# Cross-attention deviations turned ahead of the scores, context statistics paced one step sooner, one third of a pair's queries moved to the step before; the last expert's full block ahead of its short part

## The chip, the cores and the metric

The kernel runs on one core of a Trainium2 chip. Its time is device microseconds of one launch; before the change three runs gave a median of 565.46 us (563.95 to 566.39). The profile is one further execution of the same kernel, taken with the hardware profiler.

Five engines work side by side, each through its own list of instructions in the order in which it was built: PE (matrix multiply), DVE (vector), ACT (activation), POOL, and SP, which here only issues DMA. They meet through semaphores. In the profile PEld is PE's loading of weights.

## The reference, cut to what matters

One Perceiver layer on 1024 query rows (32 batches of 32, width 512), all in float32:

```python
xn  = layernorm(x)                                  # no weights
x1  = layernorm(xn) * g1 + b1;  x2 = layernorm(ctx) * g2 + b2   # ctx: 32 x 257 x 384
q   = x1 @ Wq + bq;  k = x2 @ Wk + bk;  v = x2 @ Wv + bv
x   = x + softmax(q @ k.T * 512**-0.5) @ v @ Wo + bo            # cross-attention
x   = x + self_attention(layernorm(x))              # 16 heads of 32, rotary positions
xf  = layernorm(x)
s, e = top_k(sigmoid(xf @ gate.T + bias), 2);  s = s / (s.sum(-1) + 1e-6)
x   = x + sum_j s_j * (silu(xf @ w1[e_j].T) @ w2[e_j].T)        # 8 experts, 1024 wide
```

## The kernel before, in words

**Folded weights.** The cross-attention's key weights are folded into the query weights (`mq`), its value and output weights into one (`wvo`). Scores are then taken on the raw context, and each key's reciprocal deviation (`rs`, one number for each of 257 keys) multiplies them afterwards.

**Eight steps.** A step `g` treats four batches, that is 128 query rows (tile `g` of `x_sb`). Two steps form a pair `p = g // 2`; queries are made for a whole pair. The loop at the end of the cross-attention runs `g` from 0 to 8 and overlaps neighbours: step `g` takes the scores of `g` and finishes the mixing of `g - 1`. On PE a step holds these groups:

- `pte` (L588): the weights `ex` of step `g - 1` transposed; ACT copies them to `eT` (L590).
- `pscore` (L542): the scores of `g`, from the queries `q2T` and the transposed context `nT`.
- `pc` (L599): `eT` times the context `n`; DVE evicts it to `u` (L606).
- `prs` (L557): the spread deviations `rx` of `g` transposed; ACT copies them to `rb` (L560). DVE then multiplies the scores by `rb` and takes the maximum in one custom instruction (`ex`, L563), followed by `mxq`, `nm`, ACT's exponential (L576) and DVE's product with `rb` (L579).
- `ptu` (L624), copied to `uT` (L626), and `po` (L633), which DVE adds to `x_sb` (L636).
- In even steps `pt` (L446): the next pair's normalized rows `y` transposed to `x1T`. In odd steps `pq`, `pbt` and `pb` (L475, L467, L484): the next pair's queries, three columns blocks `c` of four matmuls each. Late steps hold pieces of the self-attention's first pair instead (`spt`, `pp`).

**Statistics.** `cstats(g)` makes the deviations of step `g`: nine `bn_stats` on DVE (L505; eight on `n`, one on the last key `nl`), five small operations ending in `v` (L517), a power on POOL (`rs`, L519), and ACT's copies to `rx` and `rb` (L526, L532). It is called in step `g - 1`. `pace` holds instructions that others are to be issued after: `cstats(g)` goes after `pace["c", g]`, which before the change is the eviction `u` of step `g - 2`, executed in step `g - 1`.

**Context loads.** `load_ctx(g)` loads `n` (four DMAs of 384 KB, one per batch), `nl` (four of 48 KB) and `nT` (1542 KB), all on SP's queue; it is called three steps ahead, in `xmix(g - 3)`. Buffers: steps 2 and 5 lie in the pool `ewp`, the others alternate between two. SP waits before an issue until the buffer is free[...].

**What sets the order.** A scheduler in the framework places each engine's instructions, and DMAs on SP, from the program text, priorities and its own estimates; the text's order is not the built order. Where this document speaks of the built order, it was read from the built programs.

**Experts.** After self-attention and routing, the experts run one after the other, the fullest first. Rank `r` takes `WIDTH[r]` rows of its list: full blocks of 128 rows and a remainder that `short_part` treats in packed form (L1311 to L1317). `output` does the short part first, then the full blocks (L1397 to L1403). Each eviction `fob` is added to the rows of `out` by an indirect accumulating DMA on POOL (`add_rows`, L194). These DMAs all write `out`, so each waits for the one before. Unused places of a block point to 128 spare rows behind the 1024 real ones.

Of the kernel before, what the change touches and what calls it, by code (L numbers as in the profile page):

```python
# [9 lines left out]
F32 = mybir.dt.float32  # L10
# [7 lines left out]
P = 128  # L18
# [17 lines left out]
WIDTH = (384, 352, 288, 288, 288, 224, 192, 160)  # L36
CAP = max(WIDTH)
NB = CAP // P
EARLY = 2
Q = 32  # L40
YI, YC, YW = D, D + 8, D + 16
# [10 lines left out]
def tile_perceiver_layer(  # L52
# [138 lines left out]
        nc.vector.bn_aggr(mv, st)  # L191

    def add_rows(dst, ob, place, n):
        nc.gpsimd.indirect_dma_start(  # L194
            out=dst,
            out_offset=bass.IndirectOffsetOnAxis(ap=place, axis=0),
            in_=ob,
            in_offset=None,
            bounds_check=n * (NTT * P + P) - 1,
            oob_is_err=True,  # L200
            compute_op=ALU.add,
        )
# [22 lines left out]
    with ExitStack() as attn:  # L225
# [19 lines left out]
        with ExitStack() as xa:  # L245
# [209 lines left out]
                        )  # L455
                qs[p]["x1T"] = x1T

            def xquery(p):

                x1T = qs[p]["x1T"]  # L460
                q2T = wk.tile([P, KC, 2 * P], F32, tag="q2T", name="q2T")
                for c in range(KC):
                    if c == KC - 1:

                        pb = ps.tile([P, D], F32, tag="ps", name="pbt")
                        for k in range(KD):
                            nc.tensor.matmul(  # L467
                                pb[ts(k, Q), 0 : 2 * P], mq[:, k, DX - Q : DX], x1T[:, k, :],
                                start=True, stop=True,
                            )  # L470
                        pbs = wk.tile([P, 2 * P], F32, tag="eT", name="pbs")
                        nc.scalar.copy(pbs, pb[:, 0 : 2 * P])
                    pq = ps.tile([P, D], F32, tag="ps", name="pq")
                    for k in range(KD):
                        nc.tensor.matmul(  # L475
                            pq[:, 0 : 2 * P], mq[:, k, ts(c, P)], x1T[:, k, :],
                            start=(k == 0), stop=(k == KD - 1),
                        )
                    nc.scalar.activation(
                        q2T[:, c, :], pq[:, 0 : 2 * P], AF.Identity, bias=tcol[:, c : c + 1]  # L480
                    )
                pb = ps.tile([P, D], F32, tag="ps", name="pb")
                for i in range(2):
                    nc.tensor.matmul(  # L484
                        pb[:, i : i + 1], pbs[:, ts(i, P)], copies[:, 0, 0, Q - 1 : Q],
                        start=True, stop=True,
                    )
                qb = spool.tile([P, 2], F32, tag="qb", name="qb")
                nc.vector.tensor_scalar_add(qb, pb[:, 0:2], tcol[:, KC : KC + 1])
                qs[p]["q2T"], qs[p]["qb"] = q2T, qb  # L490

            def xbias(p):
                for i in range(2):
# [53 lines left out]
                        )  # L547
                gs[g]["pscore"] = pscore

            def xweights(g):  # L550

                p, i = g // 2, g % 2
                qb, rb, pscore = qs[p]["qb"], gs[g]["rb"], gs[g]["pscore"]

                pr = ps2.tile([P, 2, P], F32, tag="pt", name="prs")
                for c in range(2):
                    nc.tensor.transpose(  # L557
                        pr[:, c, :], gs[g]["rx"][:, c].rearrange("p b q -> p (b q)"), ident
                    )
                nc.scalar.copy(rb[:, 0:NK], pr.rearrange("p c k -> p (c k)"))  # L560
                ex = wk.tile([P, S], F32, tag="ex", name="ex")
                mx = spool.tile([P, 1], F32, tag="mx", name="mx")
                top = nc.vector.tensor_tensor_reduce(  # L563
                    out=ex, in0=pscore[:, 0:S], in1=rb, scale=1.0, scalar=-3.0e38,
                    op0=ALU.mult, op1=ALU.max, accum_out=mx,
                )
                if g % 2 or g == 0:
                    pace["x", p + 1 + g % 2] = top.ins
                mq_ = spool.tile([P, 1], F32, tag="mq", name="mxq")
                nc.vector.tensor_tensor(mq_, mx, qb[:, i : i + 1], ALU.add)  # L570
                nm = spool.tile([P, 1], F32, tag="nm", name="nm")
# [21 lines left out]
            def xmix(g):  # L593

                n, nl, ex, eT = gs[g]["n"], gs[g]["nl"], gs[g]["ex"], gs[g]["eT"]
                pc = ps.tile([P, D], F32, tag="ps", name="pc")
                for c in range(2):
                    for b in range(4):
                        nc.tensor.matmul(  # L599
                            pc[ts(b, T), 0:DC],  # L600
                            eT[:, c, ts(b, T)],
                            n[:, b, c, :],
                            start=(c == 0), stop=(c == 1),
                        )
                u = wk.tile([P, DC], F32, tag="u", name="u")
                mixed = nc.vector.scalar_tensor_tensor(  # L606
                    u, nl, ex[:, NK : NK + 1], pc[:, 0:DC], op0=ALU.mult, op1=ALU.add
                )
# [20 lines left out]
            def xout(g):  # L629
                uT = gs[g]["uT"]  # L630
                po = ps.tile([P, D], F32, tag="ps", name="po")
                for c in range(KC):
                    nc.tensor.matmul(  # L633
                        po, uT[:, c, :], wvo[:, c, :], start=(c == 0), stop=(c == KC - 1)
                    )
                nc.vector.scalar_tensor_tensor(  # L636
                    x_sb[:, g, :], po, gs[g]["rc"], x_sb[:, g, :],
                    op0=ALU.mult, op1=ALU.add,
                )


            DX = DC + 1
# [98 lines left out]
            for g in range(NTT + 1):  # L741
# [524 lines left out]
    def tails_of(m):  # L1266

        return [(0, 2 * Q)] * (m // (2 * Q)) + [(m // Q * Q - Q, Q)] * (m // Q % 2)
# [34 lines left out]
    def short_part(hT, w2, q, place, sh):  # L1303
# [13 lines left out]
        add_rows(out.rearrange("r (n w) -> (r n) w", n=n), ob[:, 0:w], place, n)  # L1317

    def turn_rows(r, xs, n, taken, idx):

# [58 lines left out]
                nc.tensor.transpose(pt[:, k, :], t["hs"][:, ts(h * KD + k, P)], ident)  # L1379
            evac(h, t["hT"][:, h * KD : (h + 1) * KD, 0:P], pt)  # L1380

    def output(t, w2):

        hT, share, idx = t["hT"], t["share"], t["idx"]
        parts = parts_of(t["n"])
        for c, m in parts:
            if m < P:
                for r0, q in tails_of(m):
                    short_part(
                        hT[:, :, c * P + r0 : c * P + r0 + q], w2, q, *t["spread"].pop(0)  # L1390
                    )
        for c, m in parts:
            if m < P:
                continue
# [5 lines left out]
                )  # L1400
            ob = fw.tile([P, D], F32, tag="fob", bufs=3, name="fob")
            nc.vector.tensor_scalar_mul(ob, po, share[:, c : c + 1])  # L1402
            add_rows(out, ob, idx[:, c : c + 1], 1)  # L1403


    rows_of = {
# [8 lines left out]
    for r in range(1, NE):  # L1415
# [8 lines left out]
        if r == 1:  # L1424
# [139 lines left out]
```

## Time and profile before

| | |
|---|---|
| median of three runs | 565.46 us (563.95 to 566.39) |
| the profiled execution's own time | 566.19 us |
| its span in the profile | 564.5 us |
| granted PE clock over the span | 0.975 |
| busy: PE, DVE, ACT, POOL | 525.1, 254.0, 123.2, 83.5 us |
| cross-attention's overlapped steps 1 to 7 | 44.3 to 126.8 us |
| last matmul ends; last add is issued; it lands | 553.3; 554.4; 559.2 us |

The span runs from the first to the last instruction of the program; the profiled execution's own time is 1.7 us longer, for what lies around it. It was 0.7 us above the median of the three runs. In lines of groups, "x" counts instructions as the trace records them: a float32 matmul of this kernel stands as two records, so a block of four `pq` matmuls is "x8". In the timeline a line gives start, length, engine, source line, operation, what it writes and reads, and in brackets the engine's idle time before it with its releaser.

### The profile page before, as it was taken

The page shows a single profiled execution, that of the slowest core. Times are in us where ns is not written, and L with a number is a line of the kernel's source. Part 1 is how long each engine was busy: PE and PEld are TensorE (multiplying, and loading weights), DVE is VectorE, ACT ScalarE, POOL GpSimd, SP SyncE. Part 2 cuts the span into 40 slices and gives each one's busy share as a digit, 9 for nine tenths or more (in the row PEclk, how much of TensorE's full clock was granted, in tenths as well). Part 3 has the DMA queues.
Part 4 walks back from the last instruction along what each step waited for, and adds up shares of the span by engine and source line. Part 5 has one row for each costly group of instructions (what it writes and reads, how often), then busy time and mean ns, then how long its engine had stood idle before and what let it go on. Part 6 is the DMA issues. An engine that isn't in the chain of part 4 may idle for free.

```text
span 564.5 us, 11301 instructions
## 1 busy us (share of the span) xinstructions
PE 525.1 (93%) x4716; PEld 340.8 (60%) x4716; DVE 254.0 (45%) x758; ACT 123.2 (22%) x274; POOL 83.5 (15%) x120
## 2 busy tenths in 40 slices
PE   6999797999999999998969999999999999999992
PEld 3646354566584875776548456547657475768580
DVE  6657778747567765668534032203122121222220
ACT  3534444323313312212022021002011010102010
POOL 2110221110001012021302110122120202112211
PEclk9999999999999999798989999999999999999997
DMA  8999979999910002012295341657553554746421
GB/s 281 383 372 395 318 244 324 357 387 386 384 58 38 3 24 93 2 42 76 81 381 216 90 100 69 238 133 221 167 168 111 128 198 154 215 159 197 161 27 21
DMA packets 43086, 104.51 MB, mean 185 GB/s; under 512 B 3985, under 2 KB 7185, under 8 KB 42002
## 3 DMA queue, kind: packets, MB, share of 16 engines
q1 hardware_dynamic: 38434, 94.91, 46.8%
q0 software_dynamic: 4592, 8.78, 7.7%
q8 instruction: 39, 0.64, 0.5%
q14 instruction: 21, 0.17, 0.1%
HBM read 75.50 MB, written 28.18 MB: 184 GB/s over the span
## 4 chain that ended last, share of the span: by engine, by line
PE 69%; DVE 2%; issue 1%; ACT 1%; POOL 0%; POOLq 0%; ACTq 0%
PE ph L1344 18%; PE fpo L1397 15%; PE pp L380 8%; PE ppv L818 5%; PE ppo L894 4%; PE fpq L1311 4%; PE phe L1148 3%; PE poe L1162 2%; PE pg L940 2%; PE pos L875 2%; PE pqs L833 2%; PE phb L1365 1%; PE xpt L1326 1%; ACT xT L176 1%; PE fpt L931 1%
## 5 line engine op out<-in xcount | busy, mean ns | idle before, releaser
L1344 PE MATMUL ph<-xT,w 128*128 128x288 f32 (+4 forms) x448 | 100.2, 382 | 3.1 <-ACT xT L176 3.1
L1344 PEld LDWEIGHTS ph<-xT,w 128*128 128x128 f32 x448 | 79.0, 190 | 19.6 <-ACT xT L176 3.7
L1397 PE MATMUL fpo<-w,hT 128*128 128x512 f32 x192 | 84.4, 596 | 0.0
L1397 PEld LDWEIGHTS fpo<-w,hT 128*128 128x128 f32 x192 | 35.9, 190 | 43.9 <-issue 43.7
L1350 DVE TENSOR_TENSOR hT<-ph,sg 128x288 f32<-128x288 f32 (+4 forms) x56 | 23.6, 422 | 61.7 <-ACT sg L1349 61.7
L1402 DVE TENSOR_SCALAR fob<-fpo,share 128x512 f32<-128x512 f32 x12 | 9.0, 751 | 77.0 <-PE fpo L1397 77.0
L1349 ACT ACTIVATE sg<-ph 128x288 f32<-128x288 f32 (+4 forms) x56 | 21.5, 383 | 85.0 <-PE ph L1344 83.5
L505 DVE BATCH_NORM_STATS2 st<-n 128x6 f32<-128x384 f32 x64 | 32.7, 549 | 2.1 <-DMA n<-in_ctx_dram 2.1
L194 POOL DMA_INDIRECT out_dram<-fob,idx x12 | 18.5, 1542 | 93.7 <-DVE fob L1402 80.9
L176 ACT COPY xT<-xpt 128x512 f32<-128x512 f32 (+2 forms) x12 | 6.0, 496 | 112.5 <-PE xpt L1326 112.4
L894 PE MATMUL ppo<-ao,oT 128*128 128x512 f32 x64 | 30.1, 624 | 0.0
L194 POOL DMA_INDIRECT out_dram<-fob,plc x9 | 13.9, 1541 | 101.5 <-DVE fob L1316 84.9
L519 POOL TENSOR_TENSOR rs<-v,mhalf 128x9 f32<-128x9 f32 x8 | 14.4, 1798 | 80.7 <-DVE v L517 42.6
L380 PE MATMUL pp<-syT,aq 128*128 128x256 f32 x96 | 25.7, 427 | 0.0
L633 PE MATMUL po<-wvo,uT 128*128 128x512 f32 x48 | 22.4, 602 | 1.2 <-ACT uT L626 1.2
L818 PE MATMUL ppv<-av,syT 128*128 128x512 f32 x48 | 23.3, 635 | 0.0
L475 PE MATMUL pq<-x1T,mq 128*128 128x256 f32 x96 | 23.1, 385 | 0.0
L1311 PE MATMUL fpq<-w,hT 128*32 128x128 f32 (+1 forms) x576 | 22.3, 309 | 0.0
L380 PE MATMUL pp<-syT,ak 128*128 128x256 f32 x96 | 22.3, 385 | 0.0
L1032 POOL DMA_INDIRECT xs_d<-fy,pi x16 | 17.0, 1064 | 35.3 <-DVE pi L1028 21.9
L380 PEld LDWEIGHTS pp<-syT,aq 128*128 128x128 f32 x96 | 20.2, 216 | 3.3
L894 PEld LDWEIGHTS ppo<-ao,oT 128*128 128x128 f32 x64 | 12.6, 199 | 14.2 <-issue 14.0
(269 smaller groups left out, 732.5 us busy)
## 6 DMA issues: line engine op xcount, KB each, us to landing
xs_d<-zero SPq DMA_DIRECT2D x8, 2112.0 KB, 20.5
w<-in_w1T_dram SPq DMA_DIRECT2D x16, 1024.0 KB, 8.4
w<-in_w2T_dram SPq DMA_DIRECT2D x16, 1024.0 KB, 8.2
nT<-in_ctxT_dram SPq DMA_DIRECT2D x8, 1542.0 KB, 9.6
n<-in_ctx_dram SPq DMA_DIRECT2D x32, 384.0 KB, 7.0
xs<-xs_d SPq DMA_DIRECT2D x4, 528.0 KB, 9.3
x_sb<-in_x_dram SPq DMA_DIRECT2D x8, 256.0 KB, 6.7
out_dram<-x_sb SPq DMA_DIRECT2D x8, 256.0 KB, 2.0
```

What stands on the lines that cost most here:

```text
L194: nc.gpsimd.indirect_dma_start(out=dst, out_offset=bass.IndirectOffsetOnAxis(ap=place, axis=0), in_=ob, in_offset=None, bounds_check=n * ( ...
L380: nc.tensor.matmul(pp[:, i, :], w[:, k, ts(e, P)], yT[:, k, :], start=(k == 0), stop=(k == KD - 1),)
L475: nc.tensor.matmul(pq[:, 0 : 2 * P], mq[:, k, ts(c, P)], x1T[:, k, :], start=(k == 0), stop=(k == KD - 1),)
L505: nc.vector.bn_stats(st[:, r, :], n[:, r // 2, r % 2, :] if r < 8 else nl)
L633: nc.tensor.matmul(po, uT[:, c, :], wvo[:, c, :], start=(c == 0), stop=(c == KC - 1))
L818: nc.tensor.matmul(pp, st[p]["yT"][:, k, ts(i, P)], av[:, k, :], start=(k == 0), stop=(k == KD - 1),)
L894: nc.tensor.matmul(pp, st[p]["oT", i][:, k].rearrange("p b q -> p (b q)"), ao[:, k, :], start=(k == 0), stop=(k == KD - 1),)
L1311: nc.tensor.matmul(po[ts(g, Q), 0:w], hT[:, f, ts(h, Q)], w2[:, f, ts(j, w)], start=(f == 0), stop=(f == KF - 1),)
L1344: nc.tensor.matmul(ph[:, 0:n], w1[:, k, ts(f, P)], t["xT"][:, k, 0:n], start=(k == 0), stop=(k == KD - 1),)
L1349: nc.scalar.activation(sg[:, 0:n], ph[:, 0:n], AF.Sigmoid)
L1350: nc.vector.tensor_mul(hT[:, f, 0:n], ph[:, 0:n], sg[:, 0:n])
L1397: nc.tensor.matmul(po, hT[:, f, ts(c, P)], w2[:, f, :], start=(f == 0), stop=(f == KF - 1),)
```

## The change

It has five parts.

1. **Deviations ahead of the scores.** The transposes `prs` and their copy to `rb` leave `xweights` for a new function `xdev(g)`, called before `xscores(g)`.
2. **Statistics one step sooner.** `pace["c", g + 3]` becomes the addition of `po` to `x_sb` in `xout(g)`, in place of `pace["c", g + 2]` at the eviction `u` in `xmix(g)`. `cstats(3)` to `cstats(7)` may thus be issued from the end of the step before the one that held them. `cstats(2)` keeps its place after `u` of step 0.
3. **A third of the queries.** `xquery` takes a range of column blocks. Block 0 is called at the end of the even step, after `xout`; blocks 1 and 2 stay in the odd step.
4. **`xbias`** is called one step later, after `xquery` and `xnorm`.
5. **Last expert.** `output` gets `short_first`; the last expert does its full block first and its short part after, and its two DMAs are declared independent. For that the spare rows become 384, one set of 128 for each block (`ROWS`, `idx`), and the output tensor grows from 1152 to 1408 rows.

```diff
+ROWS = NTT * P + NB * P
 def add_rows(dst, ob, place, n):
-    nc.gpsimd.indirect_dma_start(
+    return nc.gpsimd.indirect_dma_start(
...
-        bounds_check=n * (NTT * P + P) - 1,
+        bounds_check=n * ROWS - 1,
-            def xquery(p):
+            def xquery(p, cs=range(KC)):
...
-                for c in range(KC):
+                for c in cs:
...
+                if cs[-1] < KC - 1:
+                    return
-            def xweights(g):
-
-                p, i = g // 2, g % 2
-                qb, rb, pscore = qs[p]["qb"], gs[g]["rb"], gs[g]["pscore"]
-
+            def xdev(g):
+
+                rb = gs[g]["rb"]
                 pr = ps2.tile([P, 2, P], F32, tag="pt", name="prs")
                 for c in range(2):
                     nc.tensor.transpose(
                         pr[:, c, :], gs[g]["rx"][:, c].rearrange("p b q -> p (b q)"), ident
                     )
                 nc.scalar.copy(rb[:, 0:NK], pr.rearrange("p c k -> p (c k)"))
+
+            def xweights(g):
+
+                p, i = g // 2, g % 2
+                qb, rb, pscore = qs[p]["qb"], gs[g]["rb"], gs[g]["pscore"]
...
-                pace["c", g + 2] = mixed.ins
+                if g == 0:
+                    pace["c", 2] = mixed.ins
...
+                pace["c", g + 3] = added.ins
...
+                    xdev(g)
                     xscores(g)
...
                     if g % 2 == 0:
                         xturn(p + 1)
-                        xbias(p + 1)
                     else:
-                        xquery(p + 1)
+                        xquery(p + 1, range(1, KC))
                         if p + 2 < NTT // 2:
                             xnorm(p + 2)
+                        xbias(p + 1)
...
                 if g:
                     xout(g - 1)
+                if g % 2 == 0 and p + 1 < NTT // 2:
+                    xquery(p + 1, range(1))
...
-        idx, pattern=[[0, NE], [0, LIST // P]], base=NTT * P, channel_multiplier=1
+        idx, pattern=[[0, NE], [P, LIST // P]], base=NTT * P, channel_multiplier=1
...
-    def output(t, w2):
+    def output(t, w2, short_first=True):
...
+        if short_first:
+            short()
         for c, m in parts:
             if m < P:
                 continue
...
+        if not short_first:
+            short()
+
+            for i, a in enumerate(adds):
+                for b in adds[:i]:
+                    tc.declare_no_dep(a.ins, b.ins, reason="rows of their own")
...
-        output(t, w2s.pop(r))
+        output(t, w2s.pop(r), r + 1 < NE)
```

More of the change, by code (lines that the diff above doesn't have):

```diff
@@ L456, in xturn @@
                 qs[p]["x1T"] = x1T
-            def xquery(p):
+            def xquery(p, cs=range(KC)):
                 x1T = qs[p]["x1T"]
-                q2T = wk.tile([P, KC, 2 * P], F32, tag="q2T", name="q2T")
-                for c in range(KC):
+                if cs[0] == 0:
+                    qs[p]["q2T"] = wk.tile([P, KC, 2 * P], F32, tag="q2T", name="q2T")
+                q2T = qs[p]["q2T"]
+                for c in cs:
                     if c == KC - 1:
@@ L489, in xquery @@
                 nc.vector.tensor_scalar_add(qb, pb[:, 0:2], tcol[:, KC : KC + 1])
-                qs[p]["q2T"], qs[p]["qb"] = q2T, qb
+                qs[p]["qb"] = qb
             def xbias(p):
@@ L635, in xout @@
                     )
-                nc.vector.scalar_tensor_tensor(
+                added = nc.vector.scalar_tensor_tensor(
                     x_sb[:, g, :], po, gs[g]["rc"], x_sb[:, g, :],
@@ L1316, in short_part @@
         nc.vector.tensor_scalar_mul(ob[:, 0:w], po[:, 0:w], sh)
-        add_rows(out.rearrange("r (n w) -> (r n) w", n=n), ob[:, 0:w], place, n)
+        return add_rows(out.rearrange("r (n w) -> (r n) w", n=n), ob[:, 0:w], place, n)
     def turn_rows(r, xs, n, taken, idx):
@@ L1380, in turn_hidden, with short @@
             evac(h, t["hT"][:, h * KD : (h + 1) * KD, 0:P], pt)
-    def output(t, w2):
+    def output(t, w2, short_first=True):
         hT, share, idx = t["hT"], t["share"], t["idx"]
         parts = parts_of(t["n"])
[L1386 to L1391, printed above, removed]
+        adds = []
+        def short():
+            for c, m in parts:
+                if m < P:
+                    for r0, q in tails_of(m):
+                        adds.append(
+                            short_part(
+                                hT[:, :, c * P + r0 : c * P + r0 + q],
+                                w2, q, *t["spread"].pop(0),
+                            )
+                        )
+        if short_first:
+            short()
         for c, m in parts:
@@ L1402, in output @@
             nc.vector.tensor_scalar_mul(ob, po, share[:, c : c + 1])
-            add_rows(out, ob, idx[:, c : c + 1], 1)
+            adds.append(add_rows(out, ob, idx[:, c : c + 1], 1))
+        if not short_first:
[3 more added lines that the diff above has]
+                    tc.declare_no_dep(a.ins, b.ins, reason="rows of their own")
     rows_of = {
@@ L1557 @@
     args["out"] = nc.dram_tensor(
-        "out_0_dram", (NTT * P + P, D), F32, kind="ExternalOutput"
+        "out_0_dram", (ROWS, D), F32, kind="ExternalOutput"
     ).ap()
```

## The prediction, made before the changed kernel had run

> **What bounds the kernel now.** Read first the page's busy line, then PE's waits from 40 to 140 us, then PE's timeline of one step, then the context tile's view and the table by stage. PE is busy for 93% of the span:
>
> ```profile
> PE 525.1 (93%) x4716; PEld 340.8 (60%) x4716; DVE 254.0 (45%) x758; ACT 123.2 (22%) x274; POOL 83.5 (15%) x120
> ```
>
> So time is won only where PE waits, and a wait added ahead of PE costs its full length. The change touches two places: the cross-attention's steps (44.3 to 126.8 us) and the last 12 us. In the first, PE's waits (total us, times, longest) are:
>
> ```profile
> PE prs L557 <- ACT rx L526: 4.3, 3, 1.9
> PE ptu L624 <- DVE u L606: 2.1, 2, 1.7
> PE pc L599 <- ACT eT L590: 1.9, 2, 1.7
> PE po L633 <- ACT uT L626: 1.2, 2, 1.0
> ```
>
> That is 9.5 us; 1.0 of it (`po` of step 8) isn't touched, which leaves 8.5. Step 3 on PE shows the form:
>
> ```profile
> 66.45 0.38 PE L588 MATMUL pte<-ident,ex 128*128 128x128 f32 x2
> 66.76 1.51 PE L542 MATMUL pscore<-nT,q2T 128*32 128x257 f32 x24
> 68.08 1.47 PE L599 MATMUL pc<-n,eT 128*32 128x384 f32 x16
> 71.44 0.44 PE L557 MATMUL prs<-ident,rx 128*128 128x128 f32 x2 [1.88 <-ACT rx L526]
> 71.72 1.03 PE L475 MATMUL pq<-x1T,mq 128*128 128x256 f32 x4
> ```
>
> `prs` stands third, behind 2.7 us of `pscore` and `pc`, and still waits 1.88 us for `rx`. The deviations are late; where `prs` stands is not the cause. `rx` waits for POOL's power, and that for DVE's statistics:
>
> ```profile
> 69.16 1.80 POOL L519 TENSOR_TENSOR rs<-v,mhalf 128x9 f32<-128x9 f32 x1 [10.88 <-DVE v L517]
> ```
>
> From the end of `v` to `prs` this is 0.1 + 1.8 + 0.4 + 0.1 = 2.4 us. The statistics need the context `n`, and here the DMA queue is full: the table by stage gives for steps 1 and 2 (last columns PE clock, DMA share, GB/s), and the tile's view the time from issue to landing:
>
> ```profile
> 44.27:56.88 12.61, 12.61 (x91) 8.04 (x90) 11.01 (x32) 4.41 (x11) 1.06 (x1) 1.00 1.01 393
> 56.88:66.45 9.57, 7.53 (x63) 3.79 (x61) 6.71 (x18) 5.50 (x13) 1.39 (x2) 1.00 0.91 310
> DMA to landing us min/median/max: 3.3/7.0/14.8
> ```
>
> The 14.8 us is the last of the four loads of `n(3)`: issued at 49.6, landed at 64.3; the first two landed at 60.6 and 62.2. DVE began `cstats(3)` at 62.5, just after.
>
> [...] at 82.6 us `eT` starts only after `rx` and `rb`, which waited for POOL until 82.2. [...] The landings agree; between 44 and 66 us they follow the issues at about 0.39 MB a microsecond. [...] The trace shows such waits (up to 4.8 us), and independent spare rows are what lets the last two adds go without one.
>
> **The change part by part.** In the built order every step begins `pte`, `prs`, `pscore`, `pc` (steps 5 and 7: `prs` after 5 and 9 of 12 score matmuls). I walk the steps with each engine's built order and the durations of the trace before.
>
> *Removed and added instructions:* none but order. A block of four `pq` costs 1.8 us (1.99 less overlap); one block moves from steps 1, 3, 5 to 0, 2, 4. PE's sum stays. Behind `pt` in step 0 it waits for nothing: `x1T` ends at 45.5, and its fourth matmul starts at 45.6. So step 1 starts at 46.1 (before 44.3) and step 2 at 57.0 (before 56.9): cost 0.
>
> *`prs` first, step 2.* `cstats(2)` keeps its pace after `u`, which DVE now runs after the scores' maximum and two `bn_stats` of 0.6 on `x_sb`, at 49.8 (before 47.4). Two `bn_stats` (0.48) and the product bring it to 51.8, six more and `nl` to 55.2, the small ones to 56.1; POOL takes the pair's power (0.7) first, then this (1.8): 58.6. `rx` ends at 59.0, so `prs` waits from 57.3 to 59.1: 1.8 us. Queued behind it on PE are `pscore` and `pc`; on ACT `rx` holds back two `y` (1.5) and `eT`, so `pc` starts at 60.9 (before 60.4). The old wait of 1.67 on `eT` has only changed its name.
>
> *Statistics sooner, step 2.* DVE's built order now has three `bn_stats` on `n(3)` ahead of the maximum of step 2, the fourth and fifth ahead of `u`. The third needs the second load of `n(3)`. But SP's built order puts all four loads of `n(5)` ahead of `nT(4)` and `n(3)`; before it was two. That is 0.79 MB more in a full queue, 2.0 us: the second load lands at 64.2 (60.6 + 2, 62.2 + 2 for the first two), the third at 65.2. DVE waits; maximum 64.4, `u` 65.8 to 66.4, `ptu` 66.4 (before 62.6). PE waits 4.1 us in place of 0.37. Then `pt` 0.9, `uT` (after the exponential, as built) 67.7, `po` 2.7, moved `pq` 1.8: step 3 starts at 72.2, before 66.45 + 1.8: 3.9 late.
>
> *Step 3.* DVE ends `cstats(3)` at 70.7, `rx` 73.0: `prs` waits 0.5 in place of 1.88. No other wait; seven `bn_stats` of `n(4)` (landed by 71.8 as before) end at 74.7, when the scores do. Step 4 starts at 83.6, before 81.0: 2.6 late.
>
> *Step 4.* POOL gives `rs` at 82.4, so `prs` waits for nothing. But ACT's order now has `rx`, `q2T`, two `y` and two `pair` (3.0 us) ahead of `eT`, which ends at 86.4; `pc` waits 1.0. On DVE two `xrow` additions wait for the `y` reads, one `row` addition for `pair`; with the addition to `x_sb` and two `bn_stats` the maximum comes at 87.7, `u` at 89.0 to 89.6, `ptu` waits 1.7 (before 1.70). Step 5: 95.5 against 90.5 + 1.8: 3.2 late.
>
> *Steps 5 to 7.* `v` of 5 and 7 is built behind DVE's addition of the `po` that closes the step before, so `rx` comes 2.3 to 3.2 us into the step: `prs` waits 1.6 and 2.0, with `pscore`'s rest, `pc` and, in 7, `pp` behind it, which used to fill that time (1.39, 1.03). Step 6: `uT` behind the exponential, `po` waits 1.1 (0.25). Starts of 6, 7, 8: 107.9, 116.2, 131.7 against 104.7, 112.4, 126.8: **4.9 late**. In sum 14 us of waits against 8.5; the rest of the difference is rounding of 0.1 a step.
>
> *`xbias` later:* four DVE additions of 0.6 beside waiting time; where they matter (step 4) they are counted.
>
> *Last expert.* PE ends at 553.3 either way. Before:
>
> ```profile
> 553.36 0.75 DVE L1402 TENSOR_SCALAR fob<-fpo,share 128x512 f32<-128x512 f32 x1 [6.68 <-PE fpo L1397]
> 554.38 1.54 POOL L194 DMA_INDIRECT out_dram<-fob,idx  x1 [5.89 <-DVE fob L1402]
> ```
>
> Its add lands at 559.2, 4.8 after issue. After: `fpo` ends 1.9 earlier, its add is issued at 552.4 and lands at 557.3. The short eviction takes 0.35 (553.75); POOL is free at 554.0; a short add lands 3.4 after issue: 557.4 to 557.6 behind the other's packets. **Saved 1.6 us**; bounds 0.4 (the short add takes 4.8 after all) and 1.9 (both overlap fully). `fpo` starting right after `ph` needs the last `hT` only in its eighth pair, 6 us later: 0.
>
> **Sum:** +4.9 - 1.6 = +3.3 us. Self-attention starts that much later and PE runs through, so nothing returns it. Against the profiled execution's own 566.19 us: 569.5. That execution stood 0.7 above the median of the runs shown, 565.46; so 568.8.
>
> **Rivals.**
> - *`n(3)` is in time* (a load lands by 61 us, or DVE's gap is filled): step 2's `ptu` waits 0.8, step 4 starts at 80.4, 3.2 less late, and the rest follows. +1.7 - 1.6: 565.6. For it: the loads' issue times could shift. Against: 393 GB/s and the built order of SP.
> - *The waits go* (ends faster): DVE gets so far ahead that `rx` is ready when `pte` ends in each step. Then the 4.3 us of `prs` and 0.25 of `po` vanish and `pc` and `ptu` keep theirs: -4.5 - 1.6: 559.3. It decides where `v` ends 2.4 us before a step does. For it: from step 3 on `cstats` may start a step sooner, and DVE is busy 69 of 96 us here. Against: `v` of 5 and 7 stands behind `po`'s addition in the built order, and `n(3)` can't come sooner.
> - *More is late:* `nT(7)` now goes ahead of `n(6)` on SP, 4 us of queue; if `n(6)` and `n(7)` miss their earlier `bn_stats` too, 2 us each more: 573.
>
> A built order that left the old one standing is excluded: it has changed on four engines.
>
> **How the numbers follow.** About 0.5% (2.8 us) is what a measurement of this kernel can tell from no change. Chances: the walk 0.50, `n(3)` in time 0.27, waits go 0.15, more late 0.08. The walk's centre lies 0.5 us beyond the bound; it leaves out every wait that it doesn't list, so I count 0.36 of its 0.50 as slower, 0.14 as no change. The second gives 0.22 no change, 0.03 faster, 0.02 slower; the third 0.14 faster, 0.01 no change. Slower 0.46, same 0.37, faster 0.17. The walk's own range is 566.5 to 571; with the others, the tail's bounds and 2 in 10 left out, 561.5 to 572.5.
>
> **What would show it.** Right: `ptu` of step 2 idle about 4 us for `u`, DVE just before it idle for DMA `n`; `prs` waits of 1 to 2 us in steps 2, 5, 7; step 8's `pte` near 131.7; `n(3)` landing from 62.6; the last short add landing near 557.5 plus the delay. Wrong: DVE waits on `n` below 1 us, or PE's waits on `rx` gone.

## The result, and the profile after

The changed kernel took 572.29 us (median; 569.67 to 574.14) where the kernel before took 565.82 beside it: ratio 1.0119, interval 1.0082 to 1.0156, that is 6.5 us slower. Executed again on a chip together with other kernels it took 570.43 against 565.53: ratio 1.0087 (1.0055 to 1.0118), 4.9 us slower. The forecast was 568.8, 3.3 us slower than the shown median. The direction held, and so did the range, whose upper end was 572.5; the size was too small.

PE is as full as before, so the loss must again be read from its waits. First the busy line of the changed kernel's page, then its PE waits from 40 to 140 us (total us, times, longest; `po` of step 8 lies outside):

```profile
PE 530.1 (93%) x4716; PEld 343.9 (60%) x4716; DVE 254.3 (45%) x758; ACT 123.0 (22%) x274; POOL 83.4 (15%) x120
```

```profile
PE prs L560 <- ACT rx L531: 5.1, 4, 1.7
PE ptu L633 <- DVE u L614: 3.8, 2, 2.1
PE po L642 <- ACT uT L635: 0.7, 1, 0.7
PE pc L607 <- ACT eT L598: 0.6, 1, 0.6
```

That is 10.2 us against 8.5 for the same waits before; the forecast had 14. The timeline of step 2, cut to PE and DVE, shows the wait that the prediction put in the middle of its sum:

```profile
62.44 1.50 PE L607 MATMUL pc<-n,eT 128*32 128x384 f32 x16
62.51 1.55 DVE L510 BATCH_NORM_STATS2 st<-n 128x6 f32<-128x384 f32 x3 [2.81 <-DMA n<-in_ctx_dram]
...
63.97 0.41 DVE L571 CUSTOM_DVE_ANT_0 ex<-pscore,rb 128x257 f32<-128x257 f32 x1
...
65.41 0.60 DVE L614 SCALAR_TENSOR_TENSOR u<-nl,ex,pc 128x384 f32<-128x384 f32 x1
...
66.06 0.33 PE L633 MATMUL ptu<-ident,u 128*128 128x128 f32 x1 [2.13 <-DVE u L614]
```

DVE stands 2.81 us before the first of three `bn_stats` on `n(3)` (the forecast had it stand at the third); the maximum (`ex`) and `u` are behind them in DVE's order, and PE's `ptu` waits for `u`. The table by stage for step 2 (PE clock, DMA share, GB/s last) shows the same full queue as before:

```profile
58.75:71.62 12.87, 9.20 (x70) 5.31 (x69) 9.78 (x27) 5.29 (x13) 2.65 (x2) 1.00 0.94 325
```

At the end, POOL's last two adds and DVE's eviction ahead of the last one:

```profile
559.80 1.54 POOL L195 DMA_INDIRECT out_dram<-fob,idx  x1 [15.99 <-DVE fob L1424]
561.88 1.54 POOL L195 DMA_INDIRECT out_dram<-fob,plc  x1 [0.54 <-DVE fob L1329]
```

```profile
561.25 0.35 DVE L1329 TENSOR_SCALAR fob<-fpq,shq 128x128 f32<-128x128 f32 x1 [1.73 <-PE fpq L1324]
```

PE ends at 560.61 and the span at 570.6: 10.0 us, against 11.2 before (553.31, 564.5). The tail saves 1.2. Over all profiles below, this time is 10.0 to 10.6 us in thirteen of the fourteen with the new tail (11.5 in one) and 11.0 to 11.2 in the six without it.

The second execution of the same kernel differs in step 2. DVE's first statistics of `n(3)` there, and PE behind them:

```profile
63.52 1.02 DVE L510 BATCH_NORM_STATS2 st<-n 128x6 f32<-128x384 f32 x2 [5.02 <-DMA n<-in_ctx_dram]
```

```profile
67.26 0.90 PE L633 MATMUL ptu<-ident,u 128*128 128x128 f32 x3 [4.51 <-DVE u L614]
67.95 1.91 PE L447 MATMUL pt<-ident,y 128*128 128x128 f32 x8
```

The load was later, the wait was 4.5 us, and behind it PE's instructions are longer than elsewhere in the steps: three `ptu` 0.90 us where 0.55 is usual, eight `pt` 1.91 where 1.04. The table by stage gives that step a PE clock of 0.90, not 1.00:

```profile
57.55:74.37 16.82, 10.76 (x71) 6.60 (x69) 9.85 (x27) 5.95 (x15) 3.23 (x2) 0.90 0.89 312
```

PE busy 10.76 for the work that took 9.20 in the first profile: 1.56 us went to the clock, which stood at half from 67.1 to 70.5 us. Such a stretch at half clock is named *a stretch* below.

Behind the steps the two profiles differ in the clock too. The table by stage for self-attention and routing, first of the kernel before, then of the first and the second profile of the changed one (PE clock third from the end):

```profile
137.00:256.00 119.00, 116.33 (x1915) 81.86 (x1916) 79.21 (x164) 28.94 (x55) 14.05 (x29) 0.96 0.25 93
256.00:310.00 54.00, 47.67 (x682) 33.58 (x681) 28.63 (x118) 12.44 (x23) 11.52 (x19) 0.91 0.50 192
...
137.00:256.00 119.00, 115.34 (x1922) 82.86 (x1922) 76.64 (x162) 29.51 (x57) 10.60 (x27) 0.96 0.28 103
256.00:310.00 54.00, 47.66 (x659) 30.94 (x658) 29.45 (x108) 11.54 (x21) 11.03 (x18) 0.84 0.50 188
...
137.00:256.00 119.00, 114.98 (x1946) 80.95 (x1945) 80.15 (x167) 30.98 (x60) 12.49 (x28) 1.00 0.32 115
256.00:310.00 54.00, 47.63 (x663) 31.74 (x662) 29.73 (x117) 11.29 (x20) 9.88 (x17) 0.84 0.47 178
```

### The profile page after: what moved, and what is told of

It is laid out like the page before. It is cut to its first block, busy times and chain, and to the rows that moved or that the text cites. A ratio compares the mean times of both kernels' runs of the same rounds, so it can differ in the third digit from the quotient of the medians.

```text
span 570.6 us, 11309 instructions
## 1 busy us (share of the span) xinstructions
PE 530.1 (93%) x4716; PEld 343.9 (60%) x4716; DVE 254.3 (45%) x758; ACT 123.0 (22%) x274; POOL 83.4 (15%) x120
## 4 chain that ended last, share of the span: by engine, by line
PE 69%; DVE 2%; issue 1%; ACT 1%; POOL 0%; POOLq 0%; ACTq 0%
PE ph L1357 17%; PE fpo L1419 15%; PE pp L381 8%; PE ppv L831 5%; PE ppo L907 4%; PE fpq L1324 4%; PE phe L1161 2%; PE poe L1175 2%; PE pg L953 2%; PE pqs L846 2%; PE pos L888 1%; PE phb L1378 1%; PE xpt L1339 1%; PE fpt L944 1%; ACT xT L177 1%
## 5 line engine op out<-in xcount | busy, mean ns | idle before, releaser
L907 PE MATMUL ppo<-ao,oT 128*128 128x512 f32 x64 | 30.7, 634 | 0.0
L195 POOL DMA_INDIRECT out_dram<-fob,plc x9 | 13.9, 1541 | 91.6 <-DVE fob L1329 74.5
```

Source lines behind the costliest of these rows:

```text
L195: return nc.gpsimd.indirect_dma_start(out=dst, out_offset=bass.IndirectOffsetOnAxis(ap=place, axis=0), in_=ob, in_offset=None, bounds_chec ...
L907: nc.tensor.matmul(pp, st[p]["oT", i][:, k].rearrange("p b q -> p (b q)"), ao[:, k, :], start=(k == 0), stop=(k == KD - 1),)
```

## The experiments

One number compares all profiles: the time from `pms`, the folding's last product, to the `pte` of step 8. It leaves out what happens ahead of the steps, where `pms` starts anywhere between 42.9 and 44.8 us in kernels whose code is equal up to there. PE's busy time between the same two points is 75.2 us before. A stretch adds 1.5 to 2 us to it; so, up to 2.2 us without any stretch, does `prs` where it is built into the row of scores or of `pc`. Whether there was a stretch is therefore read from the clock of the table by stage.

| kernel | pms to step 8, us | PE busy | longest wait | a stretch | ratio to before (interval) |
|---|---|---|---|---|---|
| before | 83.71 | 75.19 | 1.88 | no | |
| changed | 86.70 | 76.48 | 2.13 | no | 1.0119 (1.0082 to 1.0156) |
| changed, again | 89.88 | 77.81 | 4.51 | yes | 1.0087 (1.0055 to 1.0118) |
| tail alone | 83.72 | 75.20 | 1.88 | no | 0.9983 (0.9962 to 1.0004) |
| changed without tail | 87.08 | 76.48 | 2.5 | no | 1.0113 (1.0080 to 1.0146) |
| block of `pq` alone | 83.86 | 76.71 | 2.07 | yes | 1.0004 (0.9981 to 1.0027) |
| deviations alone | 86.44 | 77.42 | 2.24 | yes | 1.0036 (1.0015 to 1.0056) |
| pace alone | 86.61 | 76.93 | 2.86 | yes | 1.0030 (1.0009 to 1.0052) |
| changed, `pq` back | 89.93 | 78.20 | 3.47 | yes | 1.0065 (1.0044 to 1.0086) |
| changed, old pace | 86.83 | 77.42 | 1.54 | no | 1.0045 (1.0022 to 1.0068) |
| changed, deviations back | 87.55 | 76.34 | 6.18 | yes | 1.0101 (1.0065 to 1.0138) |
| changed, `xbias` back | 88.99 | 77.94 | 3.50 | yes | 1.0094 (1.0062 to 1.0127) |
| tail and `pq` | 83.87 | 76.72 | 2.07 | yes | 0.9992 (0.9973 to 1.0011) |
| changed, loads in order | 87.67 | 78.13 | 2.12 | yes | 1.0078 (1.0053 to 1.0103) |
| the same, `xbias` back | 86.02 | 76.49 | 2.12 | no | 1.0066 (1.0037 to 1.0095) |
| loads in order, deviations back | 81.79 | 74.87 | 1.63 | no | 0.9987 (0.9965 to 1.0008) |
| the same, `xbias` back | 81.77 | 74.86 | 1.62 | no | 0.9986 (0.9965 to 1.0007) |
| loads in order, tail and `pq` | 84.84 | 76.72 | 2.07 | yes | 1.0031 (1.0011 to 1.0052) |
| before, `u` six times in step 4 | 88.65 | 76.87 | 5.93 | yes | 1.0094 (1.0062 to 1.0125) |
| deviations back, in order, `u` six times in step 2 | 88.05 | 76.92 | 6.05 | yes | 1.0086 (1.0052 to 1.0120) |

**The parts apart.** Each kernel takes the named hunks of the diff and leaves the others. Tail alone:

> The kernel before with the last expert's part alone changed (short block last, spare rows of their own, adds that don't wait for each other); cross-attention as before. Theory A (the loss lies in the cross-attention's steps, the tail gives a little back): 1.2 to 1.6 us faster than before, about 564.4; first step starts at 44.3 within 0.5 us, step 8 at 126.8, granted clock 0.975. Rival B (the untouched 1.7 us ahead of the steps and the lower clock of 0.970 come with the larger output or the moved adds): the first step starts at 45.5 to 46, clock 0.970, and the kernel is 1 to 3 us slower than before.

1.0 us faster by the ratio (-2.1 to +0.2), which alone doesn't tell it from no change; but the profile has 10.1 us from PE's end to the span's end in place of 11.2. That is A, just under its size. `pms` at 44.09 and clock 0.979: rival B falls.

Cross-attention alone (the hunks of `output` and `ROWS` undone):

> The changed kernel with the last expert's part as before; all cross-attention edits stay. Theory A: 4.2 to 4.6 us of waits and delays more than before at the end of the steps when both are counted from the end of the folding, of which 3.0 in the steps and the rest from the same clock as in the changed kernel; total 569 to 574 us, that is 1.2 us above the changed kernel on the same chip. Rival B (the loss comes with the tail's larger output): 1 us from before, 565 to 567.

6.4 us slower, and 87.08 in the steps. The loss comes with the cross-attention's edits, though only 3.4 us of it shows within the steps of this profile.

The moved block alone (`xquery` split, nothing else):

> The kernel before with the moved third of the queries alone. Its built order already puts all four loads of n(5) ahead of n(3); the statistics keep their old pace. Theory A (the old pace doesn't need n(3) in step 2, so the late load costs little; the wait of rx stays): steps 1 to 8 last as before within 1 us (82.5 less the 1.8 of the moved block at the start, plus 1.8), total 565 to 567. Rival D (the moved block alone makes the loss, by the load order): 2 to 4 us slower than before, with DVE's waits on n in step 2 or 3 above 3 us. Rival E (the block fills the waits it was moved to, at the old pace): 1 to 2 us faster, since prs in odd steps waits less than 4.3 us in sum.

No DVE wait on `n` shows, and the total is within 0.3 us of before. The steps took 83.86 with a stretch of 1.5 in step 2; without it 82.4. In the steps E is right, in the total A.

Deviations alone, pace alone, and the changed kernel without one of its edits:

> The kernel before with the deviations' transposition alone moved ahead of the scores. Counted from the folding's last product (pms) to the start of step 8, before has 83.71 us and the changed kernel 86.70. Theory A (prs first holds pscore and pc behind a late rx): 85.5 to 86.5, PE's waits of prs on rx 7 to 10 us in sum in place of 4.3, with waits of pc on eT down; total 1.8 to 2.8 us slower. Rival F (the earlier statistics are the cost): 83.5 to 84.3, total within 0.6 us. On the clock, theory H (the moved block of queries lowers the granted clock, since the kernels with it averaged 0.973 over their runs and those without it 0.9755): mean clock 0.975 or above.

> The kernel before with the statistics' pace alone changed (one step sooner). Theory A (a wait comes off prs, some go to u behind the statistics): 83.0 to 84.5 us from pms to step 8, total within 0.8 us. Rival F (DVE takes up loads that have not landed, and the maximum stands behind them): 85.5 to 87 us, DVE's waits on n above 3 us, total 1.8 to 3.3 us slower. Theory H: mean clock 0.975 or above.

> The changed kernel with the block of queries back in its old place, all else changed. Its built order has two loads of n(5) ahead of n(3), as before. Theory A (the moved block makes n(3) late by the load order, 1.3 us by the run with ordered loads, and fills no wait): 84.9 to 85.5 us from pms to step 8, total 1 to 2 us faster than the changed kernel. Rival J (the moved block fills waits that the other edits leave): 87 to 89. Theory H: mean clock 0.975 or above, which alone gives 1 us to the changed kernel's mean of 0.9727.

> The changed kernel with the statistics at their old pace. Theory A (prs first is the cost, the pace returns a little of it): 86.5 to 88 us from pms to step 8, prs waits on rx above 6 us in sum, total 0 to 1.3 us slower than the changed kernel. Rival F (the pace is the cost): 83.7 to 85, total 1.5 to 3 us faster than the changed kernel. Theory H: mean clock 0.974 or below.

Each edit alone costs some 1.3 us in the steps besides a stretch of 1.5, and 1.7 to 2.0 in the total; so each is a cost, the deviations as A has it, the pace as F has it but smaller (DVE's waits on `n` are 2.3 us, not 3). Without the moved block the loss in the steps grows (89.93 with a stretch, 88.4 less it): J in kind. Without the pace it stays (86.83): A. The totals say otherwise: 3.7 us slower than before without the block and 2.5 without the pace, where the whole change was 6.5 and 4.9. A profile is one execution and a total many, and the changed kernel wasn't run beside these two; how much each edit has in the total is not settled by them. Theory H on the clock falls: the mean clock was 0.9739 without the block and 0.9787 with the block and without the pace.

Adding the parts up:

> The kernel before with the tail and the moved block of queries; deviations, pace and xbias as before. In the runs so far the tail gives 1.2 us, and the block, once the 1.5 us that one stretch at half clock took from that profile is left out, 1.3 us in the steps (82.4 from pms to step 8 in place of 83.7). Theory A2 (the two add up): 2.2 to 2.8 us faster than before, ratio near 0.9955; 82.2 to 82.6 us from pms to step 8, without stretches at half clock. Rival N (the block gives nothing, its gain was a reading of one profile): 1.0 to 1.4 us faster, 83.6 to 84.

> The changed kernel with the deviations' transposition back behind the mixture, all else changed. From pms to step 8, stretches at half clock left out: before 83.7, changed 86.7; alone, the block gives -1.3, the deviations +1.2, the pace +1.4. Theory A2 (the parts add up): 83.5 to 84.1, total 0.8 to 1.4 us faster than before with the tail. Rival L (with the block moved, the pace is free and the deviations are the whole loss): 82.2 to 82.9. Rival M (the pace makes DVE's maximum late whatever stands first on PE): 85.5 to 87, DVE's waits on n above 2 us.

> The changed kernel with the four additions of xrow back behind the turn of x, all else changed. Theory A2 (the parts add up, and the additions cost about nothing alone): 84.7 to 85.3 us from pms to step 8, stretches at half clock left out; the rest of the changed kernel's 86.7 is then what the later additions cost by the order that they bring on DVE and ACT. Rival O (the additions cost nothing in this company either; the parts don't add up): 86.4 to 87.2.

Tail and block give 0.5 us faster (-1.5 to +0.6), not 2.5: the same stretch at 64 to 68 us eats the block's gain. The other two miss every additive figure: M for the deviations, and with `xbias` back not less but as much. The parts don't add up. No run has `xbias` alone; in the built order it changes hardly anything by itself, while in company each edit changes the order on DVE and ACT.

The changed kernel again:

> The changed kernel itself, again, for its spread. Its first profile holds 1.7 us of lateness ahead of the steps and two stretches at half clock more than the kernel before. Theory A3 (both are chance, and the change's own cost is 3.0 in the steps less 1.2 at the end): the first product after the folding starts at 43.8 within 0.5, the mean clock over the runs is 0.975, and the total is 1.5 to 3 us slower than before, ratio 1.003 to 1.005. Rival P (the lower clock belongs to the change): mean clock 0.973 or below, 4 to 7 us slower.

Neither: the mean clock was 0.976, equal to that of before, and the loss 4.9 all the same; its profile, in the result section, has a longer wait in step 2 and a stretch behind it.

**The order of loads.** In the kernels that have the block, the early statistics and so the late `n(3)`, DVE waits 2.8 to 5.4 us on `n`. (The two with the early statistics but not the block, where SP issues `n(3)` sooner, wait 2.3 and 3.3.) This edit makes SP issue `n(3)` ahead of `nT(4)` and `n(5)` (`lastn` is the last of the four loads of `n`, kept in what `load_ctx` returns):

```
-                    gs[g + 3] = load_ctx(g + 3)
+                    with tc.issue_after(gs[g + 2]["lastn"]):
+                        gs[g + 3] = load_ctx(g + 3)
```

> The changed kernel with one order more: the loads of context 4 are issued after those of context 3, and so on, so that SP issues n(3) ahead of nT(4) and of n(5). Theory A (in step 2 the statistics, and behind them maximum, u and ptu, wait for n(3)): DVE's wait of 2.8 us on n in step 2 goes, ptu of step 2 waits under 0.8 us in place of 2.13, step 3 starts 23.0 to 23.4 us after step 1 in place of 23.81, and the kernel is 1 to 2 us faster than the changed one. Rival C (step 2 is held by rx and eT, whatever n does): ptu's wait moves to prs, step 3 starts 23.6 to 24 us after step 1, no change within 0.5 us.

> The changed kernel with the deviations' transposition back in its old place and the loads of each context issued after those of the one before it. Without that order it has 87.5 us from pms to step 8, of which some 3 are stretches at half clock, and DVE waits 5.4 us on n. Theory A4 (the earlier statistics meet the late n(3), and that is their cost): DVE's waits on n under 0.5 us, ptu of step 2 under 1.5, 81.5 to 83.5 us from pms to step 8 (stretches at half clock left out), 1.5 to 3.5 us faster than before. Rival Q (the wait moves to prs, as in the changed kernel with ordered loads): 84 to 86, no faster than before by over 0.5.

> The kernel before with the tail, the moved block, the earlier statistics and the ordered loads; deviations and xrow's additions as before. Theory A4: 81.5 to 83.5 us from pms to step 8, stretches at half clock left out; 1.5 to 3.5 us faster than before. Rival Q: 84 to 86. Whether the additions matter shows against the run with them: under 0.7 us if they don't.

> The changed kernel with xrow's additions back behind the turn of x and the loads in order. Without the order it has 89.0 us from pms to step 8, 1.5 of it at half clock, and DVE waits 4.2 us on n. Theory A4: DVE's waits on n under 0.5, 82.5 to 84.5 us from pms to step 8 (stretches at half clock left out), total 1.5 us faster than before to 0.5 slower. Rival Q: 85.5 or more, 1.5 us slower or more, with the waits of prs on rx above 6 us in sum.

> The kernel before with the tail, the moved block and the ordered loads; the statistics keep their old pace. Theory A4 (at the old pace nothing waits for n(3), so its order is worth nothing): 82.0 to 82.8 us from pms to step 8, stretches at half clock left out (82.4 without the order), total within 0.6 us of that kernel, 565.2. Rival R (the order is worth something by itself, whatever the pace): below 81.5. Rival S (it costs, through the later nT and weights): 83.3 or more.

In none of the five does DVE wait on `n`. With the deviations first, the gain is lost again. In the changed kernel with ordered loads, `ptu` of step 2 waits 0.79 us and step 3 starts 22.5 us after step 1 in place of 23.81: so far theory A, and C falls. But PE's waits are now

```profile
PE prs L560 <- ACT rx L531: 5.8, 4, 2.1
PE ptu L633 <- DVE u L614: 2.5, 2, 1.7
```

`prs` waits more, in step 7 2.12 us in place of 1.69, and a stretch follows there. With `xbias` back and no stretch the steps take 86.0: Q. With the deviations in their old place, the pair without and with the order is (PE waits, and for the first the DVE wait)

```profile
PE ptu L630 <- DVE u L611: 7.3, 2, 6.2
...
DVE st L510 <- DMA n<-in_ctx_dram: 5.4, 2, 5.0
```

```profile
PE ptu L630 <- DVE u L611: 2.7, 2, 1.6
PE pc L604 <- ACT eT L595: 2.5, 2, 1.2
PE po L639 <- ACT uT L632: 1.5, 2, 1.0
PE prs L562 <- ACT rx L531: 1.1, 1, 1.1
```

and 87.55 becomes 81.79 (1.0101 becomes 0.9987): A4 in the steps, but not in the total, where 1.5 to 3.5 us less than before was expected and 0.7 was measured (-2.0 to +0.5). With `xbias` back it is the same, 81.77: the additions cost nothing here. So two things each keep the loss in the steps up: `n(3)` late under early statistics, and `prs` first. Mending one uncovers the other (1.0078, 1.0101); mending both brings 0.9987. Those two kernels with 81.8 beat the changed one by about 1%, but not the kernel before by more than the measurement tells, though their steps are 1.9 shorter and their tail 1.2. In the profile some of it comes back in self-attention, where PE stands 1.46 us within `pos`, at 158.6 to 160.0, for a reason that no view names (the kernel before runs these 128 in one go).

At the old pace the order costs (rival S: 83.3 in the steps less a stretch): `prs` of step 7 waits 2.0 in place of 1.0.

**A wait that is longer.** In the table no row whose longest wait is 1.9 us or less has a stretch in the steps; of those with 2.07 or more, ten of thirteen have one, not counting the last two rows, which test it. In two of the ten it stands behind a shorter wait of the same kernel, 1.74 and 1.86. Wait by wait: of eleven of 2.07 to 3.5 us six have a stretch behind them, and both above 4 us. That goes together; whether the wait is the cause is for the next edit: `for _ in range(6 if g == 3 else 1):` ahead of the product `u` (in the other kernel `g == 1`).

> The kernel before, with the product u of step 4 computed six times into the same tile in place of once (five more DVE instructions of 0.55 us ahead of ptu; the result stays). PE's wait for u in step 4 grows from 1.7 to about 4.4 us; some of the later statistics are moved too. Theory V (a long wait brings a stretch at half clock behind it): a stretch below full clock within 8 us behind ptu of step 4, PE busy 76.5 to 76.9 us from pms to step 8 in place of 75.2, mean clock over the runs 0.002 to 0.003 below that of before, total 4 to 5 us slower. Rival W (the stretches come by themselves): no stretch there, PE busy 75.2, equal mean clock, total 2.2 to 3.2 us slower.

> The same in step 2 of the kernel that has ordered loads, the early statistics, the moved block and the tail, with the deviations in their old place, which had no stretch in the steps, a longest wait of 1.6 us, and 81.8 us from pms to step 8: u of step 2 six times. Theory V: a wait of 4.2 to 4.6 us of ptu in step 2 and a stretch below full clock within 8 us behind it, PE busy 76.2 to 76.6 in place of 74.9, total 4 us slower or more than that kernel's 565.2. Rival W: no stretch, PE busy 74.9, total 2.2 to 3.2 us slower than that kernel.

The wait grew by 4.2 us and more, not 2.7 (DVE's built order puts the maximum and other work of the step between the repetitions), so the totals decide nothing; the profile does. PE in step 4 of the kernel before, then with `u` six times:

```profile
86.62 0.55 PE L624 MATMUL ptu<-ident,u 128*128 128x128 f32 x3 [1.70 <-DVE u L606]
87.01 1.04 PE L446 MATMUL pt<-ident,y 128*128 128x128 f32 x8
```

```profile
91.86 0.90 PE L624 MATMUL ptu<-ident,u 128*128 128x128 f32 x3 [5.93 <-DVE u L606]
92.56 1.91 PE L446 MATMUL pt<-ident,y 128*128 128x128 f32 x8
```

Same instructions, and the clock at half from 88.6 to 95.5 us, half of that in the wait and 3.6 us behind it: from the start of `ptu` to the next `pte` 5.58 us in place of 3.84, 1.7 more. The other kernel shows the same figures behind its `ptu` (0.90, 1.91). The mean clock over the executions was 0.972 and 0.971, against 0.9775 of the kernel before beside them. V holds for waits of 6 us, where the clock fell by more than V had; the second profile of the changed kernel, with 4.5, agrees. Between 2.07 and 3.5 us a stretch came in six cases of eleven; what decides there was not tested.

## Why the prediction was right and where it was wrong

The walk of starts can be laid over both profiles of the changed kernel, each counted from its `pms` (the prediction's from 43.09, the first profile's from 44.83, the second's from 43.63):

| step | 1 | 2 | 3 | 4 | 5 | 6 | 7 | 8 |
|---|---|---|---|---|---|---|---|---|
| forecast | 3.0 | 13.9 | 29.1 | 40.5 | 52.4 | 64.8 | 73.1 | 88.6 |
| first | 3.0 | 13.9 | 26.8 | 38.6 | 50.0 | 62.9 | 71.1 | 86.7 |
| second | 3.0 | 13.9 | 30.7 | 41.7 | 53.2 | 66.1 | 74.3 | 89.9 |

- *`prs` first, step 2* (forecast wait 1.8): 1.54 in the first. Right. That the edit only renames a wait is right for step 2; from step 3 on it is a loss of its own: with ordered loads, putting the deviations back turns 1.0078 into 0.9987.
- *Statistics sooner, step 2* (forecast 4.1 on `ptu`, 3.9 later at step 3): 2.13 and 4.51. The mechanism is the one named, full queue, SP's order, maximum and `u` behind a `bn_stats`; the ordered loads remove it. One load held back work that doesn't need it: in the first profile DVE began `ex` (63.97) and `u` (65.41), which don't read `n(3)`, only behind the `bn_stats` that had stood 2.81 us for it; in the second they stood 5.02 us. The size depends on two times that aren't tied to each other. On the span's own clock `u` ended at 66.0 and 67.2, near the forecast 66.4; but PE came to it at 63.9 and 62.8 where the forecast had 62.3, because the steps began 1.7 and 0.5 us late. So the first profile's 2.13 is small by chance: lateness ahead of the steps was absorbed in this wait. The second step 2, less its stretch, lasts 15.3 us, 3.9 more than before with the moved block (9.57 + 1.8).
- *Step 3, step 4*: forecast waits 0.5, 0, 1.0, 1.7; measured in the first 0.68, 0, 0.60, 1.71.
- *Steps 5 to 7*: forecast 1.6, 1.1, 2.0; measured 1.22, 0.67, 1.69. Too long by 0.3 to 0.4 each. Against that, a term of nothing was wrong: the prediction noted that `prs` stands within `pscore` in steps 5 and 7 and gave it no cost but the wait. PE in step 7, before and after:

```profile
112.69 1.51 PE L542 MATMUL pscore<-nT,q2T 128*32 128x257 f32 x24
114.02 1.47 PE L599 MATMUL pc<-n,eT 128*32 128x384 f32 x16
```

```profile
116.22 1.49 PE L547 MATMUL pscore<-nT,q2T 128*32 128x257 f32 x18
119.39 0.44 PE L560 MATMUL prs<-ident,rx 128*128 128x128 f32 x2 [1.69 <-ACT rx L531]
119.76 0.42 PE L547 MATMUL pscore<-nT,q2T 128*32 128x257 f32 x3
119.78 0.51 PE L607 MATMUL pc<-n,eT 128*32 128x384 f32 x1
120.00 0.39 PE L547 MATMUL pscore<-nT,q2T 128*32 128x257 f32 x3
120.13 1.56 PE L607 MATMUL pc<-n,eT 128*32 128x384 f32 x15
```

  From the first score to the rest of `pc` it takes 3.91 us, less the wait 2.22, where `pscore` and `prs` in one piece take 1.33 + 0.28: 0.6 lost, twice, which is most of the 1.3 us more that PE is busy (76.48 against 75.19). In step 2, where `prs` waits too but stands ahead of the whole row, the same reckoning gives 0.1; that speaks for the place within the row as the cost, not the wait.
- *Tail* (forecast 1.6): 1.2. From the last add's issue to the span's end it is 8.7 us in place of 10.1, the 1.4 less that was worked out; but its issue is 1.27 us after PE's end in place of 1.07, because the short eviction begins 0.6 after the last matmul.
- *The sum.* On the span's own clock step 8 begins at 131.53 in the first profile and at 133.51 in the second, 1.56 of that the stretch; the forecast was 131.7, and before it was 126.80. So, less the stretch, the steps are 4.7 and 5.2 us late against +4.9 (1.7 and 0.5 of it from ahead of `pms`; counted from there it is 3.0 and 4.7), and the tail to -1.2 and -1.0 against -1.6: together 3.5 and 4.2, about the forecast's 3.3. **The step that failed is "PE runs through, so nothing returns it".** With it the sum stopped at the listed waits: each was costed at its length and TensorE's clock taken as before, so that a stretch and everything behind step 8 stood at nothing. In the second profile the stretch behind the wait of 4.51 us added 1.56. In the first, the way from step 8 to the first expert's first matmul took 171.0 us in place of 168.2, with 27 us at half clock in place of 20; in the second 167.0, with 17. So of the 6.1 us that the first profile is longer, 2.8 lie behind step 8; the second is 4.3 longer. The executions show the same: of the first six, four at a mean clock of 0.970 to 0.974 took 572.3 to 574.1 us, two at 0.976 took 569.7 and 569.8.

Whether the change brings the lower clock behind the steps stays open. From step 8 to the first expert the twenty profiles take 165.2 to 171.7 us, with 13.6 to 27.3 us at half clock, and in the second measurement the changed kernel's mean clock equals that of before. The kernel before has such a spread too: in one set of its executions the mean is 568.0 us at a mean clock of 0.972, 567.1 at 0.975, 565.5 at 0.978 and 563.9 at 0.981, some 1.4 us for each 0.003. By a straight line through each kernel's executions, the changed kernel in its second measurement stands 4.7 us above the kernel before at 0.975. The two sums above, without the stretch, explain 3.5 to 4.2 of that; the rest, 0.5 to 1.2 us, isn't located. Profiles with the moved block had `pms` on average 0.6 later, though nothing ahead of it differs in the built order, and two without the block had it 1.0 later than before; whether the block has a part in it stays open.

The rivals: none of *`n(3)` in time*, *waits go* and *more is late* came about in the changed kernel; in the first profile DVE waits on `n` once. The second came in part with ordered loads and the deviations in their old place, where `prs` waits once, 1.1, and the steps take 81.8; the total stayed near the kernel before.

## What to carry to other kernels

The statistics that were put sooner on DVE waited for their data at their new place (2.81 and 5.02 us for `n(3)` in the two profiles), and the maximum and `u`, built behind them, waited with them: look whether the transfer can be there, and in what order the queue issues it, before counting the gain. Two edits that both lengthen PE's waits can cover one another, so undoing either shows little; undo both. A wait for a load lasts from the waiting engine's arrival to the landing: forecast both. And count more than the length of a long wait on PE: here the four of 4.5 to 6.2 us each had a stretch behind them, 1.5 to 2 us more.

## What the runs showed of the hardware

In the steps TensorE's clock was lost in stretches at half clock (0.50 in the table by stage from 64 to 68 us, changed kernel with the deviations back). They were 3.4 us long, or 6.8 behind the three waits of about 6 us (5.93, 6.05, 6.18), and cost PE some 1.5 to 2 us each: 1.56 in the second profile of the changed kernel, 1.68 with `u` six times in step 4 (76.87 in place of 75.19). All four waits of 4.5 to 6.2 us had one behind them. Of the shorter ones, the wait of 2.07 us had a stretch behind it in each of the three kernels that have it (at 63 to 69 us), two stretches stood behind waits of 1.74 and 1.86, and a wait of 3.47 had none. So these runs don't show from what length on a wait has a stretch behind it, nor why the clock falls. And in step 7 of the first profile, two transposes put between score matmuls cost 0.6 us more than the 0.28 that they take behind the row (3.91 less the wait of 1.69, against 1.33 + 0.28).
